# Neighbour counts from signs made by ScalarE, neighbour masks in halves by TensorE

## The chip, the cores and the metric

One NeuronCore of a Trainium2 chip runs the whole program. The metric is the device time of one execution in microseconds; runs of one kernel are compared by their median. Engines are named as in the profile: TensorE (PE, with its weight loads PEld), VectorE (DVE), ScalarE (ACT), GpSimd (POOL), and SyncE (SP), which issues the DMAs.

## The reference

The input is 16 graphs ("elements") of 1024 nodes with 64 features each, and a dense 0/1 adjacency. Four layers follow one another; each normalizes the features, clips them at zero and adds its result to its input. The change lies in layer 0. There each node's neighbours are thinned (of more than ten, every skip-th is removed, in either direction), and for every feature three quantiles over the values of the remaining neighbours are taken and weighted:

```python
removed = nb & do_dil[..., None] & ((rank + 1) % skip[..., None] == 0)
rem = removed | jnp.swapaxes(removed, 1, 2)
adj_d = jnp.where(rem, 0.0, adj_)                     # adj_: with self loops
...
vals = jnp.where(valid[..., None], x[:, None, :, :], big)   # valid = adj_d > 0
sv = jnp.sort(vals, axis=2)
for tau, wt in zip([0.25, 0.5, 0.75], [0.25, 0.5, 0.25]):
    pos = jnp.clip(tau * (m - 1.0), 0.0)
    lo, hi = floor(pos), ceil(pos)
    agg = agg + wt * (sv[lo] * (1 - frac) + sv[hi] * frac)
```

A two-layer network on x + agg ends it. Layer 1 is a weighted mean over the adjacency, layer 2 an attention of eight heads with the adjacency as a bias, layer 3 a product with the adjacency and a weight.

## The kernel before

Nothing of size (nodes x nodes x features) is sorted. The values of each feature are ranked once per element (`ranks`, a sorting network on VectorE for two elements at a time). A rank is split by `places` into one of 64 buckets (`bk`) and a place among the 16 in it (`pw`, a power of two). For every pair of features `pair_weights` builds two tables of 128 source nodes x 8 chunks x 64 buckets x 2 features: `cw` is 1 where the bucket's number is above the node's bucket, `dw` is the difference of place words between adjacent buckets. `group` multiplies both with the neighbour mask `valid` on TensorE (512 columns, eight matmuls each): `pc` is then the number of neighbours below each bucket, `pword` the bit word of the places in it. ScalarE takes `pc` out of PSUM as `cum`, `pword` as `hi`, `c1` and `c0`.

A step (b, g, t, q) serves an element, a group of eight features, a half of the 1024 columns, and one of six positions (floor and ceiling of three quantiles); an element has 8 x 2 x 6 = 96 steps. `compare` finds the bucket by `le = cum <= krow[q]` and picks count, word and value by matmuls (`prep`, `val`); `bits` and `value` finish one and two steps later. `krow[q]` comes from `positions`: the matmul `pm` of ones with `valid` counts the neighbours, and ScalarE scales the count to the position.

`picks` is a generator over these 1536 steps. Six steps ahead of need it starts `make`, which runs `group` for the next half piece by piece; `pair_weights` is called in the halves t = 0, four times. Beside it `behind` runs `background` for the next element: a part of the ranking, and `dilate`, the thinning of the eight chunks of 128 rows. `dilate` writes two arrays to DRAM: `left_d`, the neighbours that the row itself keeps, transposed by TensorE (`pv`) and copied out by ScalarE, and `rem_d`, those that the row removes. At the end of an element `stages` prepares the next one: `places`, then `neighbours` (both arrays are read back, and VectorE writes `valid = left > rem` as one fp8 tile of 1024 columns), `positions`, and `sorted_table`. The first stage is taken twelve steps before the element's end, the second seven, the others one a step.

A second generator, `layers`, does layers 1 to 3 of the finished element. After each step of `picks` it is advanced by 0.42 units of work; so layer matmuls and copies are emitted between the steps. The tile framework then orders the instructions of each engine by priority and readiness when the program is built; `adjoining` keeps the matmuls of one group together. Buffers come from small rotating tags: `b2` (six buffers, shared by sort, thinning and masks), `a2` (four), `cw` (eight, for `cw` and `dw`), and in PSUM `pa`, `pb` and `pc` with two banks each.

After the last step the layers of the last element run alone.

Of the kernel before, what the change touches and what calls it, by code (L numbers as in the profile page):

```python
# [29 lines left out]
TOP = 2.0 ** 23  # L30
MID = 1600.0
UP = 4096.0
BASE = 1032.0
LOW = 2048.0


# [1 line left out]
def tile_preln_adj_stack(  # L38
# [54 lines left out]
    def b2_(name, shape=(P, 512), dt=F32):  # L93
        return sb.tile(list(shape), dt, tag="b2", bufs=6, name=name)
# [53 lines left out]
    nc.vector.tensor_copy(rev, rev_a)  # L148
    rev_d = dram.tile([P, C], HP, name="rev_d")
    nc.sync.dma_start(rev_d, rev)  # L150
    not_i = const.tile([P, P], BF, name="not_i")
    nc.vector.tensor_scalar(not_i, identf, -1.0, 1.0, op0=OP.mult, op1=OP.add)

# [5 lines left out]

    dif_k = const.tile([P, P], BF, name="dif_k")  # L160
    nc.vector.scalar_tensor_tensor(dif_k, fmp, 2.0, identf, op0=OP.is_equal, op1=OP.subtract)
    nc.vector.tensor_scalar(dif_k, dif_k, KHI, None, op0=OP.mult)
    nc.vector.memset(dif_k[:, 0:2], 0.0)
    less_h = const.tile([P, P], HP, name="less_h")
    nc.vector.tensor_scalar(less_h, identf, -LOW, None, op0=OP.mult)
# [102 lines left out]
    nc.vector.memset(mid_c[:, 0:1], MID)  # L268
    nc.vector.memset(mid_c[:, 1:2], MID * LOW)
    nc.vector.memset(mid_c[:, 2:3], -MID)  # L270


    up_c = const.tile([P, 3], F32, name="up_c")
    for i, shift in enumerate((-0.375, 0.375, 0.0)):
        nc.vector.memset(up_c[:, i : i + 1], BASE + shift)

    sel_q = const.tile([P, NQ, 2 * BKW], BF, name="sel_q")
    for q in range(NQ):
# [158 lines left out]
    def dilate(b):  # L437

        left_d = dram.tile([C, P, N], BF, name="left_d")
        rem_d = dram.tile([C, P, N], HP, name="rem_d")
        for c in range(C):
            blk = slice(c * P, (c + 1) * P)
            nb = b2_("nb", (P, N), BF)
            nc.vector.tensor_scalar(nb, adj_rows(b, c), 0.0, None, op0=OP.is_gt)
            nc.vector.tensor_tensor(nb[:, blk], nb[:, blk], not_i, OP.mult)
            cum = b2_("cumn", (P, N), HP)  # L450
            nc.vector.tensor_tensor_scan(cum, nb, nb, 0.0, OP.add, OP.max)
            m = cum[:, N - 1 : N]
            do = small("do", [P, 1])
            nc.vector.tensor_scalar(
                do, m, float(T_THRESH), mask[:, b * C + c : b * C + c + 1], op0=OP.is_gt, op1=OP.mult
            )
            mi = small("mi", [P, 1], I32)
            nc.vector.tensor_scalar(mi, m, 1.0, None, op0=OP.add)
            nc.vector.tensor_scalar(mi, mi, 1, None, op0=OP.logical_shift_right)


            sk = small("sk", [P, 3])
            nc.vector.tensor_scalar(sk[:, 0:1], mi, 1.0, do, op0=OP.add, op1=OP.mult)
            nc.vector.tensor_scalar(sk[:, 1:2], sk[:, 0:1], -1.5, 1.5, op0=OP.mult, op1=OP.add)
            nc.vector.tensor_scalar(sk[:, 2:3], sk[:, 0:1], 0.5, -0.5, op0=OP.mult, op1=OP.add)
            act(cum, cum, AF.Abs, bias=sk[:, 1:2])
            yield
            rem = b2_("rem", (P, N), HP)
            nc.vector.tensor_scalar(rem, cum, sk[:, 2:3], None, op0=OP.is_equal)
            nc.vector.tensor_tensor(rem, rem, nb, OP.mult)  # L470
            nc.sync.dma_start(rem_d[c], rem)
            nc.vector.tensor_tensor(nb, nb, rem, OP.subtract)
            nc.vector.tensor_tensor(nb[:, blk], nb[:, blk], ident, OP.add)
            yield
            pt = pb("pv", (P, C, P), BF)
            adjoining(
                nc.tensor.transpose(pt[:, j, :], nb[:, j * P : (j + 1) * P], ident)
                for j in range(C)
            )
            left = b2_("left", (P, C, P), BF)  # L480
            nc.scalar.copy(left, pt)
            nc.sync.dma_start(left_d[:, :, blk].rearrange("c p i -> p c i"), left)
            yield
        yield left_d, rem_d

    def neighbours(left_d, rem_d):
        valid = sb.tile([P, C, N], F8, tag="valid", bufs=1, name="valid")
        for j in range(C):
            left = b2_("left", (P, N), BF)
            nc.sync.dma_start(left, left_d[j])  # L490
            rem = b2_("rem", (P, N), HP)
            nc.sync.dma_start(rem, rem_d[j])
            nc.vector.tensor_tensor(valid[:, j, :], left, rem, OP.is_gt, saturate=False)  # L493
        return valid

    def ranks(V):

# [99 lines left out]
    def positions(valid):  # L597

        m1 = sb.tile([P, N], I16, tag="m1", bufs=1, name="m1")
        for t in range(NH):
            pm = pa("pm")
            adjoining(
                nc.tensor.matmul(
                    pm, ones, valid[:, j, t * 512 : (t + 1) * 512], start=j == 0, stop=j == C - 1
                )
                for j in range(C)
            )  # L610
            nc.vector.tensor_scalar(m1[:, t * 512 : (t + 1) * 512], pm, -1.0, None, op0=OP.add)
        yield None
        krow = []
        for q in range(NQ):

            krow.append(sb.tile([P, N], HP, tag="krow", bufs=NQ, name="krow"))
            act(
                krow[q], m1, AF.Identity, scale=(q // 2 + 1) / 4.0, bias=up_c[:, q % 2 : q % 2 + 1]
            )
            if q < NQ - 1:  # L620
                yield None
        n6 = a2("n6", (P, N), I16)
        nc.vector.tensor_scalar(n6, m1, q_tau, q_add, op0=OP.mult, op1=OP.add)
        nc.vector.tensor_scalar(n6, n6, 2, None, op0=OP.logical_shift_right)
        kq = sb.tile([P, N], HP, tag="kq", bufs=1, name="kq")
        nc.scalar.copy(kq, n6)
        yield krow, kq
        nr = a2("nr", (P, N), I16)
        nc.vector.tensor_scalar(nr, m1, r_tau, None, op0=OP.mult)
        nc.vector.tensor_scalar(nr, nr, 3, None, op0=OP.bitwise_and)  # L630
        coef = sb.tile([P, N], BF, tag="coef", bufs=1, name="coef")
        nc.vector.tensor_scalar(coef, nr, w_frac, w_one, op0=OP.mult, op1=OP.add)
        yield coef
# [33 lines left out]
    def pair_weights(c0, bk, pw):  # L667


        sh = [P, C, NBK, 2]  # L670
        ib = bc(iota_b[:, None, :, :], sh)
        b_ = bc(bk[:, :, None, c0 : c0 + 2], sh)
        cw = sb.tile(sh, BF, tag="cw", bufs=8, name="cw")
        nc.vector.tensor_tensor(cw, ib, b_, OP.is_gt)
        eq = a2("eq", sh, BF)
        nc.vector.tensor_tensor(eq, ib, b_, OP.is_equal)
        nc.vector.tensor_tensor(at[:, :, 1:, :], eq, bc(pw[:, :, None, c0 : c0 + 2], sh), OP.mult)
        dw = sb.tile(sh, BF, tag="cw", bufs=8, name="dw")
        nc.vector.tensor_tensor(dw, at[:, :, 1:, :], at[:, :, :NBK, :], OP.subtract)  # L679
        return cw, dw  # L680

    def group(g, t, bk, pw, valid, weights):
# [2 lines left out]

        hs = slice(t * 512, (t + 1) * 512)
        cum = tb("cum", (P, 4, 512), HP)
        c1 = tb("c1", (P, 4, 512), HP)  # L690
        c0 = tb("c0", (P, 4, 512), HP)
# [7 lines left out]
        for pp in range(4):  # L699
            if t == 0:  # L700
# [1 line left out]
            cw, dw = (w.rearrange("p c b s -> p c (b s)") for w in weights[pp])  # L702
            pc = pc_("pc")
            adjoining(
                nc.tensor.matmul(pc, cw[:, j, :], valid[:, j, hs], start=j == 0, stop=j == C - 1)  # L705
                for j in range(C)
            )
            act(cum[:, pp, :], pc, AF.Identity, bias=up_c[:, 2:3])
            if late is not None:
                low_part(*late)  # L710
            pw_ = pc_("pword")
            adjoining(
                nc.tensor.matmul(  # L713
                    pw_, dw[:, j, :], valid[:, j, hs], start=j == 0, stop=False, skip_group_check=True
                )
                for j in range(C)
            )
# [9 lines left out]
    def picks():  # L727
# [8 lines left out]
        weights, tables, state, vs_of, els = {}, {}, {}, {}, {}  # L736

        def make(el, g, t):
            gen = group(g, t, el.bk, el.pw, el.valid, weights)
            tables[el.b, g, t] = next(gen)  # L740
            return gen

        def compare(n):
# [2 lines left out]
            hs = slice(t * 512, (t + 1) * 512)  # L746
            cum, c1, c0 = tables[b, g, t]
            le = a4("le", (P, 4, 512), HP)
            nc.vector.tensor_tensor(le, cum, bc(el.krow[q][:, None, hs], [P, 4, 512]), OP.is_le)  # L749
            wa = a4("wa", (P, 4, 512), HP)  # L750
            nc.vector.tensor_tensor(wa, le, c0, OP.mult)  # L751
            wb = a4("wb", (P, 4, 512), HP)
# [66 lines left out]
        for _ in make(els[0], 0, 0):  # L819
            yield 0.1  # L820
        coming = behind = stages = iter(())
        last, per = len(steps), NG * NH * NQ
        for n in range(last + 2):
            b, g, t, q = steps[min(n, last - 1)]
            to_go = per - n % per
            if n < last:
# [3 lines left out]
                if to_go == 2 * NQ and b + 1 < B:  # L830
# [3 lines left out]
                        pass  # L834
                    els[b + 1] = arrive(b + 1)
                    stages = els[b + 1].stages
                    next(stages)
                if to_go <= NQ:
                    next(stages, None)
                if q == 0 and n + NQ < last:  # L840
                    coming = make(els[steps[n + NQ][0]], *steps[n + NQ][1:3])
            if 0 <= n - 1 < last:
                bits(n - 1)
            next(coming, None)
            if to_go == NQ + 1:
                next(stages, None)
            if 0 <= n - 2:
                value(n - 2)
                if (n - 1) % per == 0:
# [81 lines left out]
    def stages(el):  # L931
# [4 lines left out]
        nc.sync.dma_start(rk, rk_d[:, :, rows])  # L936
        el.bk, el.pw = places(rk)
        yield
        el.valid = neighbours(*thinned.pop(b))
        where = positions(el.valid)  # L940
        next(where)
        yield
        vs = q4("vs")
        nc.sync.dma_start(vs[rows, :], vs_d[rows, :])
        table = sorted_table(s, vs)
        for q in range(NQ - 1):
            next(where)
            if q == 2:
                next(table)
            yield  # L950
        el.krow, el.kq = next(where)
        el.tab = next(table)
# [253 lines left out]
```

## Time and profile before

| | |
|---|---|
| runs, median of 3 | 13935.4 us (13928.6 to 13939.7) |
| profiled execution, its time | 13956.7 us |
| its span | 13954.9 us |
| mean granted TensorE clock | 0.978 |
| TensorE busy | 12582.4 us, 90% |
| VectorE busy | 12588.9 us, 90% |
| ScalarE busy | 8441.5 us, 60% |
| DMA | 842 MB, 18.9% of the 16 engines |

The first step of an element begins when its first `le` (line 749) starts. The first of all starts at 323.9 us; before that the ranking and thinning of element 0 run with nothing beside them. From 13589 us on only the layers of the last element run. In between an element takes some 840 us. Rows of the profile give a line, an engine, an operation, the tiles as out<-in, the form, the count, then busy time and the mean duration of one, then the idle time before it and what ended it. ScalarE's activations and copies made through the helper `act` all have line 373, so they are told apart by their tiles.

### The profile page before, as it was taken

What the parts mean: (1) busy time and instruction counts of PE and PEld (TensorE: products, weight loads), DVE (VectorE), ACT (ScalarE), POOL (GpSimd) and SP (SyncE); (2) the same over time, 40 slices, a digit from 0 to 9 for tenths busy, and PEclk for the clock granted to TensorE, in tenths of its full rate; (3) what the DMA queues carried; (4) which work ended last, traced back from release to release, by engine and by line L of the source; (5) the groups of instructions that cost most, each with busy time, mean ns of one, the idle gap of its engine ahead of it and who ended that gap; (6) DMA issues with size and microseconds to landing.
All of it is one profiled execution on the core that took longest, in us unless ns stands there. A gap on an engine that the chain in (4) does not pass through costs nothing. (4 is left out here: it accounts for less than half of the span.)

```text
span 13954.9 us, 237846 instructions
## 1 busy us (share of the span) xinstructions
PE 12582.4 (90%) x95489; PEld 5956.5 (43%) x95489; DVE 12588.9 (90%) x22771; ACT 8441.5 (60%) x14490; POOL 24.4 (0%) x138
## 2 busy tenths in 40 slices
PE   1889999999999998999999999999989999999998
PEld 0224444444444444444444444444444444444445
DVE  9999999999998999999899998999989999878773
ACT  1446666666666665666566666666656666666656
POOL 0000000000000000000000000000000000000000
PEclk9999999999999999999999999999999999999998
DMA  3012121211212112121211212112121221201012
GB/s 98 28 35 68 46 81 50 79 55 54 75 49 85 50 55 73 52 80 51 65 59 52 87 47 78 48 60 77 48 77 49 66 68 47 90 27 61 25 43 76
DMA packets 482773, 842.39 MB, mean 60 GB/s; under 512 B 234624, under 2 KB 236800, under 8 KB 481664
## 3 DMA queue, kind: packets, MB, share of 16 engines
q1 hardware_dynamic: 481664, 827.18, 18.9%
q8 instruction: 748, 12.26, 0.4%
q14 instruction: 361, 2.96, 0.1%
HBM read 616.27 MB, written 206.57 MB: 59 GB/s over the span
## 5 line engine op out<-in xcount | busy, mean ns | idle before, releaser
L713 PE MATMUL pword<-valid,dw 128*128 128x512 fp8e4 x8192 | 1977.6, 384 | 139.0 <-DVE dw L679 101.8
L751 DVE TENSOR_TENSOR wa<-le,c 128x2048 f16<-128x2048 f16 x1536 | 1871.4, 1218 | 199.2 <-PE prep L765 170.3
L705 PE MATMUL pc<-valid,cw 128*128 128x512 fp8e4 x8192 | 1977.5, 382 | 18.6 <-DVE valid L493 14.7
L749 DVE TENSOR_TENSOR le<-cum,krow 128x2048 f16<-128x2048 f16 x1536 | 1869.4, 1217 | 36.2 <-PE val L765 36.1
L753 DVE TENSOR_TENSOR wb<-le,c 128x2048 f16<-128x2048 f16 x1536 | 1870.0, 1217 | 3.1 <-PE prep L765 3.1
L373 ACT ACTIVATE s<-s,nm 128x1024 f32<-128x1024 f32 x1024 | 1169.2, 1143 | 723.1 <-DVE nm L1099 718.9
L772 ACT COPY wi<-prep 128x512 f32<-128x512 f32 x1536 | 898.4, 585 | 773.0 <-PE prep L765 649.2
L373 ACT ACTIVATE hi<-pword,mid_c 128x512 f16<-128x512 f32 x1024 | 705.2, 689 | 1047.8 <-PE pword L718 1043.2
L713 PEld LDWEIGHTS <-dw 128*128 128x128 bf16 x8192 | 759.9, 98 | 1257.0 <-issue 220.8
L426 PE MATMUL pcols<-identf,s 128*128 128x128 f32 x8192 | 1151.9, 282 | 143.0 <-ACT s L373 93.7
L1090 PE MATMUL sp<-kT,qT 64*128 64x512 f32 x4096 | 1168.3, 646 | 123.4 <-DVE nm L1099 121.6
L705 PEld LDWEIGHTS <-cw 128*128 128x128 bf16 x8192 | 765.6, 98 | 1078.8 <-issue 252.2
L765 PE MATMUL val<-le,tab 128*32 128x512 f16 x12288 | 1136.1, 388 | 52.4 <-DVE vs L793 34.2
L426 PEld LDWEIGHTS pcols<-identf,s 128*128 128x128 f32 x8192 | 909.9, 142 | 627.0 <-ACT s L373 254.1
L793 DVE SCALAR_TENSOR_TENSOR vs<-pz,vs 128x512 f32<-128x512 f32 x1536 | 1050.1, 684 | 123.4 <-PE pz L786 96.9
L1109 PE MATMUL ao<-eT,v 128*64 128x128 f32 x16384 | 1121.5, 278 | 42.1 <-ACT eT L429 38.2
L429 ACT COPY eT<-pcols 128x512 f32<-128x512 f32 x2048 | 1108.9, 592 | 54.0 <-PE pcols L426 52.6
L373 ACT ACTIVATE cum<-pc,up_c 128x512 f16<-128x512 f32 x1024 | 707.6, 691 | 700.5 <-PE pc L705 669.2
L1109 PEld LDWEIGHTS ao<-eT,v 128*64 128x64 f32 x16384 | 920.9, 137 | 342.4 <-ACT eT L429 216.3
L373 ACT ACTIVATE vs<-val 128x512 f32<-128x512 f32 x1536 | 925.8, 603 | 203.0 <-PE val L765 106.7
L765 PE MATMUL prep<-wb,sel_w 128*32 128x512 f16 x6144 | 658.8, 395 | 204.2 <-DVE wb L753 197.8
L1099 DVE CUSTOM_DVE_ANT_0 s<-sp,ad,nm 128x512 f32<-128x512 f32 x1024 | 730.2, 746 | 88.9 <-PE sp L1090 88.3
(258 smaller groups left out, 19483.3 us busy)
## 6 DMA issues: line engine op xcount, KB each, us to landing
ad<-in_adj_dram SPq DMA_DIRECT2D x768, 512.0 KB
adjT_d<-aT SPq DMA_DIRECT2D x128, 512.0 KB
aT<-adjT_d SPq DMA_DIRECT2D x128, 512.0 KB
md<-sm SPq DMA_DIRECT2D x216, 256.0 KB
sb<-md SPq DMA_DIRECT2D x216, 256.0 KB
rem_d<-rem SPq DMA_DIRECT2D x128, 256.0 KB
left_d<-left SPq DMA_DIRECT2D x128, 256.0 KB
left<-left_d SPq DMA_DIRECT2D x128, 256.0 KB
```

Source lines behind the costliest of these rows:

```text
L373: nc.scalar.activation(out_, in_, func, **kw)
L426: nc.tensor.transpose(pt[:, c, :], ad[:, (4 * s + c) * P : (4 * s + c + 1) * P], identf)
L429: nc.scalar.copy(aT[:, 4 * s : 4 * s + 4, :], pt)
L705: nc.tensor.matmul(pc, cw[:, j, :], valid[:, j, hs], start=j == 0, stop=j == C - 1)
L713: nc.tensor.matmul(pw_, dw[:, j, :], valid[:, j, hs], start=j == 0, stop=False, skip_group_check=True)
L749: nc.vector.tensor_tensor(le, cum, bc(el.krow[q][:, None, hs], [P, 4, 512]), OP.is_le)
L751: nc.vector.tensor_tensor(wa, le, c0, OP.mult)
L753: nc.vector.tensor_tensor(wb, le, c1, OP.mult)
L765: nc.tensor.matmul(dst[32 * pp : 32 * pp + 32, :], w[pp], r[pp], start=i in (0, 3), stop=i in (2, 4), tile_position=(0, 32 * pp),)
L793: nc.vector.scalar_tensor_tensor(vs, pz, -191.0, vs, op0=OP.is_equal, op1=OP.mult)
L1090: nc.tensor.matmul(sps[e], qT[e * D : (e + 1) * D, i * P : (i + 1) * P], kT[e * D : (e + 1) * D, hs], start=True, stop=True,)
L1109: nc.tensor.matmul(ao[e * D : (e + 1) * D, :], v[:, j, e * D : (e + 1) * D], eTs[e][:, j, :], start=j == 0, stop=j == C - 1, tile_position ...
```

## The change

Three things are done together.

1. `pair_weights` subtracts once (`cw` = bucket number minus the node's bucket). `eq` is then a comparison of `cw` with zero, and ScalarE turns `cw` in place into a sign: `Sign(0.5 - cw)`, which is +1 or -1. A sum of signs over the neighbours is (total - 2 x count below), so `group` takes `cum` out of PSUM as half the sum, by a Copy with scale 0.5 instead of an Identity with a bias column, and `compare` asks `is_ge` against a `krow` in the same halves (scale 0.5 - tau, bias 0.5 or -0.25). `dif_k` changes its sign. The constant columns `up_c` go, `half_c` comes.

2. `dilate` writes `left_d` as it lies, without the transpose; `rem` is bf16. `neighbours` is called for one half of the columns at a time and yields after each of the eight chunks. For a chunk it reads four blocks of `left_d` and half a row block of `rem_d` into one tile `lr`; TensorE forms the mask in PSUM: one matmul with minus the identity on `rem`, four with the blocks of `left` as weights on the identity, which transposes them; ScalarE writes `valid` by a Relu. There are two `valid` tiles of 512 columns.

3. The stages are spread: instead of one lump seven steps before the end, a table `STEPS` says how many pieces to take at each of the last twelve steps.

```diff
+    minus_i = const.tile([P, P], BF, name="minus_i")
+    nc.vector.tensor_scalar(minus_i, identf, -1.0, None, op0=OP.mult)
...
-    nc.vector.tensor_scalar(dif_k, dif_k, KHI, None, op0=OP.mult)
+    nc.vector.tensor_scalar(dif_k, dif_k, -KHI, None, op0=OP.mult)
...
-    up_c = const.tile([P, 3], F32, name="up_c")
-    for i, shift in enumerate((-0.375, 0.375, 0.0)):
-        nc.vector.memset(up_c[:, i : i + 1], BASE + shift)
+    half_c = const.tile([P, 3], F32, name="half_c")
+    for i, shift in enumerate((0.5, -0.25, 0.5)):
+        nc.vector.memset(half_c[:, i : i + 1], shift)
...
-        rem_d = dram.tile([C, P, N], HP, name="rem_d")
+        rem_d = dram.tile([C, P, N], BF, name="rem_d")
...
-            rem = b2_("rem", (P, N), HP)
+            rem = b2_("rem", (P, N), BF)
...
-            pt = pb("pv", (P, C, P), BF)
-            adjoining(
-                nc.tensor.transpose(pt[:, j, :], nb[:, j * P : (j + 1) * P], ident)
-                for j in range(C)
-            )
-            left = b2_("left", (P, C, P), BF)
-            nc.scalar.copy(left, pt)
-            nc.sync.dma_start(left_d[:, :, blk].rearrange("c p i -> p c i"), left)
+            nc.sync.dma_start(left_d[c], nb)
...
-    def neighbours(left_d, rem_d):
-        valid = sb.tile([P, C, N], F8, tag="valid", bufs=1, name="valid")
+    def neighbours(left_d, rem_d, t):
+        hs = slice(t * 512, (t + 1) * 512)
+        valid = sb.tile([P, C, 512], F8, tag=f"valid{t}", bufs=1, name="valid")
         for j in range(C):
-            left = b2_("left", (P, N), BF)
-            nc.sync.dma_start(left, left_d[j])
-            rem = b2_("rem", (P, N), HP)
-            nc.sync.dma_start(rem, rem_d[j])
-            nc.vector.tensor_tensor(valid[:, j, :], left, rem, OP.is_gt, saturate=False)
-        return valid
+            lr = b2_("lr", (P, 2, 512), BF)
+            nc.sync.dma_start(
+                lr[:, 0, :].rearrange("i (c j) -> i c j", c=4),
+                left_d[4 * t : 4 * t + 4, :, j * P : (j + 1) * P].rearrange("c i j -> i c j"),
+            )
+            nc.sync.dma_start(lr[:, 1, :], rem_d[j, :, hs])
+            pn = pb("pn")
+            def made():
+                yield nc.tensor.matmul(
+                    pn, minus_i, lr[:, 1, :], start=True, stop=False, skip_group_check=True
+                )
+                for c in range(4):
+                    cols = slice(c * P, (c + 1) * P)
+                    yield nc.tensor.matmul(
+                        pn[:, cols], lr[:, 0, cols], ident, start=False, stop=c == 3,
+                        skip_group_check=True,
+                    )
+            adjoining(made())
+            act(valid[:, j, :], pn, AF.Relu, saturate=False)
+            if j < C - 1:
+                yield None
+        yield valid
...
-                    pm, ones, valid[:, j, t * 512 : (t + 1) * 512], start=j == 0, stop=j == C - 1
+                nc.tensor.matmul(pm, ones, valid[t][:, j, :], start=j == 0, stop=j == C - 1)
...
-        yield None
+            yield None
...
-                krow[q], m1, AF.Identity, scale=(q // 2 + 1) / 4.0, bias=up_c[:, q % 2 : q % 2 + 1]
+                krow[q], m1, AF.Identity, scale=0.5 - (q // 2 + 1) / 4.0,
+                bias=half_c[:, q % 2 : q % 2 + 1],
...
-        nc.vector.tensor_tensor(cw, ib, b_, OP.is_gt)
+        nc.vector.tensor_tensor(cw, ib, b_, OP.subtract)
         eq = a2("eq", sh, BF)
-        nc.vector.tensor_tensor(eq, ib, b_, OP.is_equal)
+        nc.vector.tensor_scalar(eq, cw, 0.0, None, op0=OP.is_equal)
+        act(cw, cw, AF.Sign, scale=-1.0, bias=half_c[:, 2:3])
...
-            act(cum[:, pp, :], pc, AF.Identity, bias=up_c[:, 2:3])
+            act(cum[:, pp, :], pc, AF.Copy, scale=0.5)
...
-            nc.vector.tensor_tensor(le, cum, bc(el.krow[q][:, None, hs], [P, 4, 512]), OP.is_le)
+            nc.vector.tensor_tensor(le, cum, bc(el.krow[q][:, None, hs], [P, 4, 512]), OP.is_ge)
...
+        STEPS = {12: 1, 11: 2, 10: 2, 9: 2, 8: 2, 7: 5, 6: 4, 5: 1, 4: 1, 3: 1, 2: 1, 1: 2}
...
-                    next(stages)
-                if to_go <= NQ:
+                for _ in range(STEPS.get(to_go, 0)):
                     next(stages, None)
...
-            if to_go == NQ + 1:
-                next(stages, None)
...
-        el.valid = neighbours(*thinned.pop(b))
+        masks = thinned.pop(b)
+        el.valid = []
         where = positions(el.valid)
-        next(where)
-        yield
+        for t in range(NH):
+            for r in neighbours(*masks, t):
+                if r is None:
+                    yield
+            el.valid.append(r)
+            next(where)
+            yield
         vs = q4("vs")
         nc.sync.dma_start(vs[rows, :], vs_d[rows, :])
         table = sorted_table(s, vs)
+        next(table)
+        yield
         for q in range(NQ - 1):
             next(where)
-            if q == 2:
-                next(table)
             yield
```

More of the change, by code (lines that the diff above doesn't have):

```diff
@@ L32 @@
 UP = 4096.0
-BASE = 1032.0
 LOW = 2048.0
@@ L605, in positions @@
             adjoining(
-                nc.tensor.matmul(
-                    pm, ones, valid[:, j, t * 512 : (t + 1) * 512], start=j == 0, stop=j == C - 1
-                )
+                nc.tensor.matmul(pm, ones, valid[t][:, j, :], start=j == 0, stop=j == C - 1)
                 for j in range(C)
@@ L682, in group @@
     def group(g, t, bk, pw, valid, weights):
-        hs = slice(t * 512, (t + 1) * 512)
         cum = tb("cum", (P, 4, 512), HP)
@@ L704, in group @@
             adjoining(
-                nc.tensor.matmul(pc, cw[:, j, :], valid[:, j, hs], start=j == 0, stop=j == C - 1)
+                nc.tensor.matmul(pc, cw[:, j, :], valid[:, j, :], start=j == 0, stop=j == C - 1)
                 for j in range(C)
             )
-            act(cum[:, pp, :], pc, AF.Identity, bias=up_c[:, 2:3])
+            act(cum[:, pp, :], pc, AF.Copy, scale=0.5)
             if late is not None:
@@ L713, in group @@
                 nc.tensor.matmul(
-                    pw_, dw[:, j, :], valid[:, j, hs], start=j == 0, stop=False, skip_group_check=True
+                    pw_, dw[:, j, :], valid[:, j, :], start=j == 0, stop=False, skip_group_check=True
                 )
@@ L738, in make @@
         def make(el, g, t):
-            gen = group(g, t, el.bk, el.pw, el.valid, weights)
+            gen = group(g, t, el.bk, el.pw, el.valid[t], weights)
             tables[el.b, g, t] = next(gen)
```

## The prediction

> A measurement of this kernel can tell about 0.2% (28 us) from no change; "faster" and "slower" below mean by more than that.
>
> **What bounds the kernel now.** I read the page's head first. TensorE and VectorE are both busy for 90% of the span, so the shares alone don't say which sets the time, and the change takes work from VectorE and gives some to TensorE.
>
> ```profile
> span 13954.9 us, 237846 instructions
> PE 12582.4 (90%) x95489; PEld 5956.5 (43%) x95489; DVE 12588.9 (90%) x22771; ACT 8441.5 (60%) x14490; POOL 24.4 (0%) x138
> ```
>
> The kernel holds its own experiment. The sort and its way back for the next pair of elements stop at 11754 us (last row of line 563) and the thinning at 12144 us (last row of line 469), while elements 14 and 15 are still to come. I asked for the busy times by element, cut where the first `le` (line 749) of each begins (columns: stretch, length, busy PE, PEld, DVE, ACT, POOL, TensorE clock, DMA share, GB/s). They are elements 4, 5, 14 and 15.
>
> ```profile
> 3524.80:4368.90 844.10, 781.89 (x5990) 370.82 (x5988) 795.31 (x1402) 530.11 (x912) 1.77 (x8) 0.98 0.20 63
> 4368.90:5197.80 828.90, 772.89 (x5919) 364.92 (x5917) 767.30 (x1427) 521.66 (x900) 1.53 (x8) 0.99 0.20 62
> 11918.70:12754.30 835.60, 783.83 (x5962) 369.97 (x5962) 697.80 (x1216) 526.24 (x904) 1.55 (x8) 0.98 0.17 53
> 12754.30:13589.00 834.70, 773.87 (x5949) 367.88 (x5947) 641.48 (x1094) 503.82 (x883) 1.49 (x8) 0.98 0.13 40
> ```
>
> The reader is to see that VectorE falls from 795 to 641 us while the element takes 829 to 844 us before and 835 after. TensorE stays at 93 to 94% of each. So **TensorE, with the waits between its bursts, sets the pace**, and VectorE's load is near to it but not above it. Elements 4 and 5 speak a little against this: 28 us of VectorE go with 15 us of time.
>
> Then I read the waits of TensorE (who waited for whom, total us, times, longest), to see what stands between its bursts and which of it the change touches.
>
> ```profile
> PE prep L765 <- DVE wb L753: 197.8, 192, 5.2
> PE pword L713 <- DVE dw L679: 101.8, 93, 3.4
> PE pcols L426 <- ACT s L373: 93.7, 116, 3.0
> PE pm L606 <- DVE valid L493: 27.7, 23, 5.0
> PE pc L705 <- DVE valid L493: 14.7, 31, 1.7
> ```
>
> Last I read the order of time around one call of `pair_weights` (start, duration).
>
> ```profile
> 4335.93 0.68 DVE L674 TENSOR_TENSOR cw<-iota_b,bk 128x1024 bf16<-128x1024 bf16 x1
> ...
> 4340.92 1.90 PE L705 MATMUL pc<-valid,cw 128*128 128x512 fp8e4 x8
> ...
> 4341.71 0.69 DVE L676 TENSOR_TENSOR eq<-iota_b,bk 128x1024 bf16<-128x1024 bf16 x1
> ...
> 4344.12 0.68 DVE L679 TENSOR_TENSOR dw<-at 128x1024 bf16<-128x1024 bf16 x1
> ...
> 4345.21 1.04 PE L713 MATMUL pword<-valid,dw 128*128 128x512 fp8e4 x4
> ```
>
> Here `cw` is made early and the eight matmuls of `pc` run before `eq` has begun; `pword` then waits for `dw`. The change breaks this order: the Sign overwrites `cw` in place, so it can't start before `eq` has read it, and `pc` comes after the Sign.
>
> **What the Trainium skill says.** "VectorE: DVE Perf Modes", The perf-mode tier table: a two-tensor operation in bf16 reaches two elements a cycle, a one-tensor operation four. The trace agrees in kind: 684 ns for the two-tensor `cw`, 479 ns for the one-tensor `rem` (line 469) of the same size. "ScalarE: Activation LUTs", What ACT_TABLE_LOAD costs: 186 ns + 0.833 ns an element, and about 93 ns for each per-partition operand. The trace: 603 ns for a Copy of 512 (estimate 613), 691 ns with a bias column (estimate 706). The same page, Table sets: cheap functions sit in every set; it names relu, copy, identity and abs there, not sign. The trace has 34 table loads of 1283 ns and none for Abs, but no Sign. "Perfetto Trace Analysis", Identifying the Most-Contended Engine: matmul busy time is no good measure of headroom, since matmuls are pipelined; hence the comparison of elements above rather than the 90%.
>
> **The change part by part.** The rows that price it (busy us, mean ns of one):
>
> ```profile
> L373 ACT ACTIVATE cum<-pc,up_c 128x512 f16<-128x512 f32 x1024 | 707.6, 691 | 700.5 <-PE pc L705 669.2 <-DVE le L749 15.9 <-DVE bit L780 4.9
> L493 DVE TENSOR_TENSOR valid<-left,rem 128x1024 fp8e4<-128x1024 bf16 x128 | 153.4, 1220 | 27.4 <-DMA rem<-rem_d 19.0 <-PE pword L713 7.9 <-issue 0.2
> L373 ACT ACTIVATE cumn<-cumn,sk 128x1024 f16<-128x1024 f16 x128 | 147.4, 1152 | 146.5 <-DVE sk L464 135.4 <-DVE sk L465 10.0 <-DMA aT<-adjT_d 0.8
> L481 ACT COPY left<-pv 128x1024 bf16<-128x1024 bf16 x128 | 129.3, 1010 | 89.8 <-PE pv L477 89.7
> L477 PE MATMUL pv<-ident,nb 128*128 128x128 bf16 x1024 | 85.8, 226 | 127.0 <-DVE nb L472 111.8 <-DVE nb L473 15.1
> L469 DVE TENSOR_SCALAR rem<-cumn,sk 128x1024 f16<-128x1024 f16 x128 | 61.3, 479 | 3.0 <-ACT cumn L373 3.0
> ```
>
> VectorE. `cw` becomes a subtraction of the same form: 684 ns, no change. `eq` becomes a one-tensor comparison with a constant. Nearest is `rem`'s 479 ns, less the per-partition scalar (lines 454 and 458 on one column take 207 and 144 ns): 479 - 60 = 420 ns. It saves 684 - 420 = 264 ns x 512 = 135 us. `valid` goes: 153 us. Together -288 us, 18 us an element. Elements 14 and 15 put this near zero; elements 4 against 5 would give 15/28 of it, -154 us. I take a tenth: **-29** (ends 0 and -154).
>
> ScalarE. Added: 512 Signs at 1152 ns (the Abs, same size, bias column) = 590 us; 256 Relus out of PSUM at 603 to 691 ns, 0.65 x 256 = 166 us. Removed: `left`, 129 us; `cum` as a Copy with a constant, 691 - 603 = 88 ns x 1024 = 90 us. Net +537 us: 60% busy becomes 64%. ScalarE isn't the bound, but TensorE waits for it in many places, about 300 us by summing its waits on ACT. If a wait grows as busy over idle (1.53 to 1.80), that is +18%, 54 us; since `cum` is also out of PSUM sooner, I take **+30** (ends 0 and +90).
>
> TensorE. Rates come from busy time over count, for the mean of a matmul includes its pipeline: 1977.6/8192 = 0.241 us for 512 columns, 85.8/1024 = 0.084 us for a transpose with its own weights. Each of the 256 masks (16 elements x 2 halves x 8) takes one of the first and four of the second; 1024 transposes of `pv` go. 256 x 0.241 + 1024 x 0.084 - 1024 x 0.084 = +62 us. TensorE idles some 7% of an element and the masks are spread over ten steps, so a fifth falls into gaps: **+50** (ends +20 and +70).
>
> The wait for masks. TensorE now stands 27.7 + 14.7 = 42 us for `valid`. Afterwards `pm` can still wait for the last Relu of each half, 32 x 0.65 = 21 us: **-22**. The mask matmuls wait for their reads (`lr`): twice as many reads as before, of half the size, in the same six-buffer tag, on SP's queue, behind which the adjacency rows of the layers are queued. VectorE waited 19 us on 21 of 128 such reads; twice as many on TensorE would be 38, none if they run ahead: **+10**. Writing `nb` as it lies instead of the transposed copy costs nothing: the 256-byte pieces move from the write to the read, and the DMA engines are 19% busy.
>
> The weights. `pword` waits for `dw` 93 times; each is 264 ns shorter: **-25**. At such places `pc` can no longer go ahead of `eq`: eight matmuls, 8 x 0.241 = 1.93 us, come after the Sign. After `eq`, `dw` needs two more operations, 2 x 684 ns = 1.37 us, the Sign 1.15 us, so both are ready about together and `pc` has lost its cover. 93 x 1.93 = 180 us if nothing else fills it, nothing if matmuls of the layers do; I take a sixth: **+30** (ends 0 and +180). Behind a Sign that waits for `eq`, ScalarE's evictions `hi`, `wi`, `vs` stand in line, and TensorE for their PSUM; that is the third rival.
>
> The start. Before the first `le` (323.9 us) nothing hides 16 Relus and the first Signs; 8 VectorE masks of 1.22 us go: **+5** (ends -10 and +15). Signs and offsets folded into constants, `is_ge` for `is_le`, bf16 for fp16 in `rem` and the steps of the stages cost nothing by themselves: same shapes, same rows.
>
> Sum: -29 + 30 + 50 - 22 + 10 - 25 + 30 + 5 = **+49 us**. The profiled execution took 13956.7 us (span 13954.9 and 1.8 around it), so 14006 by its clock. It lies 21 us above the median of the runs, 13935.4; against that, **13985 us**.
>
> **The rivals.**
> VectorE is the bound after all (faster). For it: 93 to 94% busy in elements 4 and 5, and the 28 us there that cost 15. Against: elements 14 and 15. It gives -154 + 49 + 29 = -76, about 13860, and 13755 if nine tenths of 288 us count. The other terms come to +78, so it decides from 106 us, 37% of VectorE's saving, on.
> It evens out (no change). Mask matmuls and `pc` drop into gaps that TensorE has anyway, +50 and +30 halved, and ScalarE's share hides: 49 - 25 - 15 - 30 = -21, 13914.
> ScalarE's queue blocks (clearly slower). If a third of the 512 Signs hold the queue for 1.15 us and TensorE behind it, +196 on top: 14180. For it: ACT already stands 719 us for `nm`, so its order runs into VectorE's. Against: it is idle 36%.
> The mask reads come late, 256 x 0.6 us = +154: 14140.
> The change does not do what it says: Sign is not in the loaded sets, and 512 Signs cost two loads each, 1024 x 1.283 = +1314 us: 15300.
>
> **How the numbers follow.** My forecast 0.30, VectorE 0.28, evens out 0.22, blocked queue 0.14, late reads 0.04, table loads 0.02. Slower: 0.30 + 0.14 + 0.04 + 0.02 = 0.50; no change 0.22; faster 0.28. The forecast is 13985, its own range 13964 to 14060. For 8 in 10 the range reaches through the VectorE case down to 13800 and up to 14180, leaving out the far half of that case and of the blocked queue.
>
> **What would show it.** In the changed profile: `eq` at about 420 ns, `cw` at 684; VectorE near 12300 us busy; Sign rows near 1150 ns and as many table loads as before; `cum` near 603 ns; TensorE's busy time up by some 60 us; waits of `pc` on ScalarE's `cw` in place of `pword` on `dw`; none on VectorE's `valid`. An element should take 838 to 842 us. If elements 1 to 13 fall by 10 us while 14 and 15 don't, VectorE was the bound and I am wrong; if all rise by over 15 us with ScalarE's waits on `eq`, it is the queue.

## The result, and the profile after

The changed kernel takes **13925.0 us** (median of 11 runs, 13916.7 to 13937.9) against 13938.7 us (11 runs, 13925.6 to 13962.1): ratio **0.9990, 95% interval 0.9981 to 0.9998**. That is 14 us less, half of what the prediction called the smallest difference to be told from none. The forecast was 50 us more: the sign was wrong, and the size of several terms.

The head of the changed kernel's page, its profiled execution:

```profile
span 13921.9 us, 238842 instructions
PE 12568.3 (90%) x95745; PEld 5943.7 (43%) x95745; DVE 12368.4 (89%) x22644; ACT 8885.4 (64%) x15130; POOL 27.0 (0%) x138
```

VectorE's busy time falls by 220 us, ScalarE's rises by 444, TensorE's falls by 14. The work was moved from VectorE to ScalarE as the change says; on TensorE, the new rows don't show in the sum. The rows of what came in, and one that stayed (busy us, mean ns of one, idle before it and who ended it):

```profile
L372 ACT ACTIVATE cum<-pc 128x512 f16<-128x512 f32 x1024 | 612.1, 598 | 683.0 <-PE pc L718 674.7 <-DVE bit L793 3.7 <-DVE le L762 1.6
L372 ACT ACTIVATE cw<-cw,half_c 128x1024 bf16<-128x1024 bf16 x512 | 591.0, 1155 | 80.7 <-DVE eq L688 79.8
L688 DVE TENSOR_SCALAR eq<-cw 128x1024 bf16<-128x1024 bf16 x512 | 214.1, 418 | 5.9 <-PE pz L798 5.1 <-DMA z<-w 0.4
L372 ACT ACTIVATE valid<-pn 128x512 fp8e4<-128x512 f32 x256 | 146.4, 599 | 75.8 <-PE pn L497 72.4 <-PE pword L726 1.4
L497 PE MATMUL pn<-ident,lr 128*128 128x128 bf16 x1024 | 101.6, 221 | 0.0
L492 PE MATMUL pn<-lr,minus_i 128*128 128x512 bf16 x256 | 99.2, 387 | 2.7 <-DMA lr<-rem_d 2.5
L372 ACT ACT_TABLE_LOAD x34 | 43.6, 1283 | 24.8 <-DVE rq_f L312 24.2
```

The prices hold: `eq` 418 ns (420 forecast), the Sign 1155 (1152), `cum` 598 (603), and 34 table loads as before, so Sign needs no switch. The mask reads are no wait (2.5 us).

The two profiled spans are 33 us apart, but 19 of these belong to the two executions and not to the change: the one of the kernel before took 18 us more than its median here (13956.7 against 13938.7), the one of the changed kernel 1 us less. Where the 33 us lie is seen by stage, cut at the first `le` of elements 0, 1 and 14 (columns as in the prediction). First the kernel before, then the changed one:

```profile
0.00:323.90 323.90, 39.43 (x172) 18.20 (x173) 294.77 (x738) 41.95 (x53) 1.50 (x11) 0.99 0.34 103
323.90:1034.80 710.90, 594.26 (x3572) 195.10 (x3572) 666.72 (x919) 311.34 (x498) 0.00 (x0) 0.93 0.10 32
1034.80:11918.70 10883.90, 10071.38 (x77371) 4786.90 (x77368) 10145.72 (x18352) 6835.00 (x11748) 18.82 (x104) 0.98 0.20 62
```

```profile
0.00:336.30 336.30, 39.90 (x195) 20.07 (x196) 286.92 (x737) 47.83 (x67) 1.50 (x11) 0.98 0.33 99
336.30:1008.40 672.10, 569.43 (x3569) 190.34 (x3568) 646.93 (x902) 336.96 (x535) 0.00 (x0) 0.95 0.11 34
1008.40:11899.00 10890.60, 10090.10 (x77591) 4781.07 (x77588) 9974.49 (x18248) 7196.89 (x12271) 21.38 (x104) 0.99 0.20 62
```

The start is 12 us longer, **element 0 is 39 us shorter**, and elements 1 to 13, most of the run, are 7 us longer in 10884 although VectorE is busy 171 us less in them. Element 14 gives 10 us, the rest 3. In element 0 no layers of a finished element run yet: TensorE is busy 84% there, VectorE 94%. So the profiled gain lies where VectorE is the busier of the two, and elsewhere its relief is spent on something. VectorE's load alone doesn't account for the 39 us: its busy time falls by only 20 there. A part is spread between executions: with the same work on VectorE and TensorE (the spare Signs below), element 0 took 703.5 us. The granted clock differs in it, too (0.93 and 0.95).

The elements that the prediction had compared (4, 5, 14, 15):

```profile
3507.50:4359.10 851.60, 783.78 (x5985) 369.14 (x5985) 783.43 (x1392) 555.95 (x946) 1.21 (x8) 0.98 0.20 63
4359.10:5191.40 832.30, 777.52 (x5972) 367.21 (x5972) 754.62 (x1416) 551.01 (x943) 2.10 (x8) 0.99 0.20 61
11899.00:12724.20 825.20, 772.89 (x5972) 365.97 (x5972) 681.45 (x1206) 554.72 (x945) 1.55 (x8) 0.99 0.17 53
12724.20:13556.00 831.80, 776.95 (x5958) 368.31 (x5957) 636.32 (x1096) 525.83 (x910) 1.49 (x8) 0.99 0.13 40
```

They are no shorter in 4 and 5, although VectorE now has 12 us less in each. What changed most, past the start, are TensorE's waits for the weights, the masks and the attention (who waited for whom, total us, times, longest):

```profile
PE sp L1109 <- DVE nm L1118: 189.4, 225, 3.3
PE pc L718 <- ACT cw L372: 81.5, 118, 9.4
PE pm L619 <- ACT valid L372: 9.6, 18, 1.3
```

The wait of `pword` for `dw` (102 us) and those for `valid` (42 us) are gone. In their place stand 82 us of `pc` for the Sign, and the attention's `sp` waits 68 us longer for VectorE's `nm`; before, that row was

```profile
PE sp L1090 <- DVE nm L1099: 121.6, 172, 3.9
```

How the first of these comes about, at one `pair_weights` of the changed kernel:

```profile
4747.71 0.68 DVE L686 TENSOR_TENSOR cw<-iota_b,bk 128x1024 bf16<-128x1024 bf16 x1
...
4758.35 0.42 DVE L688 TENSOR_SCALAR eq<-cw 128x1024 bf16<-128x1024 bf16 x1
4758.80 1.15 ACT L372 ACTIVATE cw<-cw,half_c 128x1024 bf16<-128x1024 bf16 x1 [1.85 <-DVE eq L688]
...
4760.01 3.21 PE L718 MATMUL pc<-valid,cw 128*128 128x512 fp8e4 x8 [1.83 <-ACT cw L372]
```

The subtraction has ended 10 us before `eq` reads it. `eq` comes late, the Sign must wait for it, ScalarE stands idle for 1.85 us and TensorE for 1.83. The 512 instructions of each kind can be paired in order of start (for `pc`, the first eight matmuls with each `cw`). Before, `pc` began ahead of `eq`'s end in 372 cases; now in none. The median from the end of the operation that makes `cw` to the start of `eq` is 6.9 us (5.7 before).

### The profile page after: what moved, and what is told of

The parts are those of the page before. It is cut to its first block, busy times and chain, and to the rows that moved or that the text cites. A ratio compares the mean times of both kernels' runs of the same rounds, so it can differ in the third digit from the quotient of the medians.

```text
span 13921.9 us, 238842 instructions
## 1 busy us (share of the span) xinstructions
PE 12568.3 (90%) x95745; PEld 5943.7 (43%) x95745; DVE 12368.4 (89%) x22644; ACT 8885.4 (64%) x15130; POOL 27.0 (0%) x138
## 5 line engine op out<-in xcount | busy, mean ns | idle before, releaser
L726 PE MATMUL pword<-valid,dw 128*128 128x512 fp8e4 x8192 | 1944.9, 380 | 18.0 <-ACT cum L372 15.8
L372 ACT ACTIVATE cum<-pc 128x512 f16<-128x512 f32 x1024 | 612.1, 598 | 683.0 <-PE pc L718 674.7
L1118 DVE CUSTOM_DVE_ANT_0 s<-sp,ad 128x512 f32<-128x512 f32 x1024 | 675.9, 684 | 161.7 <-PE sp L1109 131.5
```

The lines of the kernel that those rows point to most:

```text
L372: nc.scalar.activation(out_, in_, func, **kw)
L726: nc.tensor.matmul(pw_, dw[:, j, :], valid[:, j, :], start=j == 0, stop=False, skip_group_check=True)
```

## The experiments

Ratios are to the kernel before, run beside each version on the same chip, with 95% intervals. One limit holds for all of them: the framework orders the instructions anew for each version, so a change of load also changes the order, and no run holds the order fixed.

**The two halves of the change, and VectorE's relief alone.**

Signs alone: the kernel before with the new `pair_weights`, `cum`, `krow`, `le` and `dif_k`.

> The kernel before with the signs alone (one subtraction, eq from it, Sign by ScalarE, counts and positions in halves); thinning, masks and stages as before. VectorE does 135 us less, ScalarE 500 us more, TensorE the same. Theory A (TensorE with its waits sets the pace while layers run, so VectorE's relief shows only in element 0): elements 1 to 13 stay within 0.5% of 837 us each, element 0 falls by 10 to 20 us, the total by about 15 us (ratio 0.998 to 1.000). Rival B (VectorE's relief is worth its share everywhere and the masks' matmuls eat it): elements 1 to 13 fall by 5 to 8 us each, ratio 0.992 to 0.995. Rival C (the Sign is what costs, the masks pay for it): elements 1 to 13 rise by 4 us or more, ratio 1.003 or more.

Measured: 1.0005 (0.9996 to 1.0013).

Masks alone: the changed kernel with those edits undone.

> The changed kernel with the weights, counts and positions of the kernel before; masks in halves by TensorE and the stages spread as changed. VectorE does 153 us less, TensorE some 60 us more, ScalarE 40 us more. Theory A: elements 1 to 13 within 0.5% of 837 us, the start longer by 5 to 12 us, element 0 shorter by 15 to 25 us, ratio 0.998 to 1.000. Rival B (masks cost what VectorE's relief gains): elements 1 to 13 rise by 2 to 5 us each, ratio 1.002 to 1.006. Rival C (masks gain what the Sign costs): they fall by 4 us or more, ratio 0.994 to 0.997.

Measured: 1.0000 (0.9992 to 1.0009).

Cheap `eq`, on the kernel before:

```diff
-        nc.vector.tensor_tensor(eq, ib, b_, OP.is_equal)
+        nc.vector.tensor_scalar(eq, cw, 0.0, None, op0=OP.is_equal)
```

> The kernel before, only that eq is made by one one-tensor comparison of cw with zero (684 to 420 ns, 512 times: 135 us less of VectorE), nothing added on any other engine. It leaves out the right choice of the bucket: eq marks other buckets than it should. Theory A: elements 1 to 13 move by less than 2 us each, element 0 falls by 10 to 20 us, ratio 0.998 to 1.000. Rival B (VectorE's relief is worth its share): 135/16 = 8.4 us of each element, ratio 0.991 to 0.994.

Measured: **0.9968 (0.9956 to 0.9981)**.

`eq` twice, on the kernel before:

```diff
         nc.vector.tensor_tensor(eq, ib, b_, OP.is_equal)
+        nc.vector.tensor_tensor(eq, ib, b_, OP.is_equal)
```

> The kernel before with eq computed twice: 512 more VectorE operations of 684 ns, 350 us in all, 21.9 us an element. Theory A with VectorE just below the pace: elements 1 to 13 rise by 5 to 15 us (VectorE then is busy 816 of some 840 us and becomes the bound), element 0 by its full 22 us or more, ratio 1.006 to 1.018. If TensorE has room for it all: ratio below 1.004. Rival B (VectorE bounds already): 22 to 25 us each, ratio 1.025 or more.

Measured: **1.0112 (1.0098 to 1.0126)**.

What follows. VectorE's load does count: 135 us less gives 45 us (0.32%), a third; 350 us more costs 156 us (1.12%), 45%. (By VectorE's busy time in the profiles, 126 us less and 295 more, it is 36 and 53%.) In the profile of the cheap `eq`, element 0 is 23 us shorter, elements 1 to 13 together 32, element 14 8. Rival B had the whole of VectorE's relief; it is wrong in both runs. My theory A had next to nothing outside element 0 for the cheap `eq` (0.998 or more), and misses there; the doubled `eq` lies inside its range (1.006 to 1.018), with elements 1 to 13 longer by 9.7 us each. So near its present amount VectorE's load is worth a third to a half of itself. The intervals are 18 to 20 us wide to either side, so the third is anything from a fifth to nearly a half.

Each half of the change pays back what it gains, though the numbers that B gave for the halves didn't come: both stand at the upper end of A's range. The signs stand 0.37% above the cheap `eq`, which is all their relief and a little more; the masks relieve VectorE of 153 us and gain nothing. Each half alone shortens element 0 (693.9 and 684.7 us, from 710.9).

**What the Sign costs: ScalarE's load, or its place?**

On the kernel before, a Sign that nobody waits for:

```diff
         nc.vector.tensor_tensor(eq, ib, b_, OP.is_equal)
+        spare = sb.tile(sh, F8, tag="spare", bufs=1, name="spare")
+        act(spare, cw, AF.Sign, scale=-1.0, bias=up_c[:, 2:3], saturate=False)
```

> The kernel before, with 512 more Signs by ScalarE: each reads cw as it stands and writes a spare tile that nobody reads; nothing waits for it. ScalarE does about 590 us more, no other engine does more, no order is forced. The signs alone stood 0.37% (52 us) above the cheap eq alone. Theory L (that is ScalarE's load): ratio 1.003 or more. Theory D (that is the new order: pc behind eq and the Sign): ratio below 1.0015.

Measured: 1.0005 (0.9997 to 1.0013). 512 Signs more, 506 us of ScalarE's busy time, are free within 0.13%: theory L falls.

The signs alone without the Sign:

```diff
-        act(cw, cw, AF.Sign, scale=-1.0, bias=half_c[:, 2:3])
```

> The signs alone (masks as before), with the Sign left out, so that the counts are wrong. VectorE does 135 us less as with the cheap eq alone. Theory D (the Sign costs by its place: behind eq and ahead of pc): the 52 us between the signs alone (1.0005) and the cheap eq alone (0.9968) go, ratio 0.996 to 0.9975. If the other edits of the signs (subtraction, Copy, positions in halves) cost them: ratio 0.9995 to 1.001.

Measured: 0.9971 (0.9960 to 0.9982), the cheap `eq` again. So 0.34% of the signs' 0.37% is the Sign, and by the run above not its load: what is left is its place between `eq` and `pc`. TensorE's waits go with it: from the signs alone to this run, those of `pc` for the Sign fall from 104 us to none and those of `sp` for `nm` from 188 to 131, while `pword` waits for `dw` again, 88 us.

The changed kernel without the Sign (same edit):

> The changed kernel with the Sign left out, so that the weights are the bare differences and the counts are wrong; 590 us of ScalarE and the step between subtraction and pc go, all else stays. Theories L and D both: 40 to 60 us below the changed kernel, ratio to the kernel before 0.995 to 0.997. If it stays at 0.999, neither is the cost and the cheap eq gains only in the order of the kernel before.

Measured: 0.9990 (0.9973 to 1.0008). The interval is wide because of one of its 14 executions, 14087.8 us; the others lie between 13908.8 and 13919.3. The median of all is 13915.0 against 13944.2 of the kernel before beside it: 0.9979, some 15 us below the changed kernel, where 40 to 60 were expected. So in the changed kernel the Sign's place costs, as far as this tells, a third of what it costs in the signs alone. No run shows why.

Can the Sign be put apart from `eq`? On the changed kernel:

```diff
-        nc.vector.tensor_tensor(cw, ib, b_, OP.subtract)
-        eq = a2("eq", sh, BF)
-        nc.vector.tensor_scalar(eq, cw, 0.0, None, op0=OP.is_equal)
-        act(cw, cw, AF.Sign, scale=-1.0, bias=half_c[:, 2:3])
+        dif = a2("dif", sh, BF)
+        nc.vector.tensor_tensor(dif, ib, b_, OP.subtract)
+        act(cw, dif, AF.Sign, scale=-1.0, bias=half_c[:, 2:3])
+        eq = a2("eq", sh, BF)
+        nc.vector.tensor_scalar(eq, dif, 0.0, None, op0=OP.is_equal)
```

> The changed kernel, but the subtraction goes to a tile of its own and the Sign from there to cw, so neither has the Sign to wait for eq nor eq for anything but the subtraction. Same load on all engines. Theory D (order): the waits of pc for the Sign fall from 82 us to below 40, ratio to the kernel before 0.995 to 0.9975. Theory L (load): as the changed kernel, 0.9985 to 1.0. A third outcome: the extra tile in the four-buffer tag delays eq and others, ratio above 1.0.

Measured: 1.0064 (1.0051 to 1.0077), slower, the third outcome; the wait of `pc` for the Sign rose from 82 to 113 us instead of falling. So this run doesn't test the Sign's place, for `dif` adds one more tile to the tag `a2`. Its `eq` row, and that of the kernel before, show on what `eq` waits:

```profile
L690 DVE TENSOR_SCALAR eq<-dif 128x1024 bf16<-128x1024 bf16 x512 | 217.1, 424 | 64.4 <-PE pz L798 63.4
L676 DVE TENSOR_TENSOR eq<-iota_b,bk 128x1024 bf16<-128x1024 bf16 x512 | 350.6, 685 | 29.8 <-PE pz L785 29.5
```

`pz` makes nothing that `eq` reads. It is the reader of `bit` and `wi`, which live in the same tag `a2` of four buffers: `eq` waits for a buffer. In the kernel before there were 29.5 us of such waits, which I had passed over.

**TensorE's part in the masks.** The changed kernel with one matmul for five:

```diff
-                yield nc.tensor.matmul(pn, minus_i, lr[:, 1, :], start=True, stop=False, ...)
-                for c in range(4):
+                for c in range(1):
                     cols = slice(c * P, (c + 1) * P)
-                    yield nc.tensor.matmul(pn[:, cols], lr[:, 0, cols], ident, start=False, ...)
+                    yield nc.tensor.matmul(pn, lr[:, 0, cols], lr[:, 1, :], start=True, stop=True, ...)
```

> The changed kernel with one matmul of 512 columns a mask instead of five (both read tiles still enter it), so that the masks are wrong; TensorE does 1024 transposes of 84 ns busy time less, 57 to 86 us, all waits stay. Theory A (TensorE sets the pace in elements 1 to 13): 40 to 70 us below the changed kernel, ratio to the kernel before 0.994 to 0.996. Rival (TensorE's extra work falls into its gaps): less than 20 us below, ratio 0.9975 to 0.999.

Measured: 0.9955 (0.9943 to 0.9967), 0.35% or 49 us below the changed kernel's 0.9990. That is what theory A said. The row removed had 102 us busy, and 57 to 86 us of work were expected to go. So TensorE's work counts for a half to five sixths of its busy time: also a part, not the whole.

**The buffer.** `eq` goes into the tile that becomes `dw` two operations later, instead of one of tag `a2`. Every engine does the same work.

```diff
-        eq = a2("eq", sh, BF)
+        dw = sb.tile(sh, BF, tag="cw", bufs=8, name="dw")
+        eq = dw
...
-        dw = sb.tile(sh, BF, tag="cw", bufs=8, name="dw")
```

On the changed kernel:

> The changed kernel with eq written into the buffer that dw gets afterwards (tag cw, eight buffers) instead of a tile of tag a2 (four, shared with wi, bit, w). Same work on every engine. In the changed kernel eq starts 6.9 us (median) after the subtraction has ended, and pc never before eq has. Theory D with the buffer as the cause: eq and the Sign move ahead, the wait of pc for the Sign falls from 82 to below 40 us, ratio to the kernel before 0.9945 to 0.9975. Rival (eq is late because VectorE is full, not for its buffer): ratio 0.998 to 1.0. Third: eq early takes VectorE from more urgent work, above 1.0.

Measured: **0.9781 (0.9768 to 0.9794)**, four times the gain expected at best.

On the kernel before:

> The kernel before with eq in dw's buffer in the same way: the control for the run above. There pc waits for cw alone, so eq's place matters only for dw and pword (102 us of waits). If the buffer matters through the Sign only: ratio 0.999 to 1.001. If it frees dw as well: 0.994 to 0.998.

Measured: **0.9762 (0.9749 to 0.9776)**. So the buffer is not a matter of the Sign. Its TensorE waits:

```profile
PE sp L1090 <- DVE nm L1099: 71.7, 110, 2.6
PE pword L713 <- DVE dw L679: 6.1, 8, 1.6
```

102 us of waiting for `dw` become 6, and 122 for `nm` become 72. With the same instructions the runs are 332 us shorter (the profiled spans 341). The pairs in order of start show what moved: from the end of `cw` to the start of `eq` the median falls from 5.7 to 1.1 us, and from the end of `dw` to the first `pword` matmul that reads it, it rises from 0.9 to 15.6 us. The weights had come just when TensorE needed them, or too late; now they lie ready. So these 2.4% were waiting, not the load of an engine, and another buffer for `eq`, with the order that the framework then makes, is what removed it. The granted clock is higher too, 0.984 against 0.978 to 0.981; if all of TensorE's time went with it, that would be some 0.5% (an estimate).

What in the buffer did it stays open. The edit lets `eq` come early, and it leaves the four buffers of `a2` to `wi`, `bit` and `w`, which are on the way of every step. No run separates the two, and none gives `a2` a fifth buffer. The run with `dif` is the counterpart: one tile more in `a2`, and 0.7% slower than the changed kernel.

**What the change is worth once the buffer is free.** Masks alone and signs alone, with `eq` in `dw`'s buffer.

> The masks in halves by TensorE and the spread stages, weights and counts as before, eq in dw's buffer. Against the kernel before with eq in dw's buffer (0.9762): if VectorE's relief is now worth more than the mask matmuls cost (50 us by the run with few masks), 0.972 to 0.975; if both cancel as they did with the shared tag, 0.975 to 0.978; if the masks cost, above 0.978.

Measured: 0.9789 (0.9776 to 0.9803).

> The signs alone, masks as before, eq in dw's buffer. If the Sign's price was its place behind a late eq, it is gone now and the cheap eq gains its 0.3%: 0.972 to 0.975. If the Sign still costs: 0.977 to 0.981.

Measured: **0.9743 (0.9730 to 0.9757)**, 13581.4 us, the fastest version. The head of its page, and one of its `pair_weights` (here `dw<-cw` is `eq`):

```profile
span 13575.8 us, 237190 instructions
PE 12264.6 (90%) x94441; PEld 5881.0 (43%) x95489; DVE 12458.6 (92%) x22771; ACT 8839.2 (65%) x15002; POOL 24.5 (0%) x138
```

```profile
4499.40 0.68 DVE L675 TENSOR_TENSOR cw<-iota_b,bk 128x1024 bf16<-128x1024 bf16 x1
4500.11 0.43 DVE L678 TENSOR_SCALAR dw<-cw 128x1024 bf16<-128x1024 bf16 x1
...
4500.57 1.15 ACT L373 ACTIVATE cw<-cw,half_c 128x1024 bf16<-128x1024 bf16 x1 [0.58 <-DVE dw L678]
...
4524.77 1.89 PE L708 MATMUL pc<-valid,cw 128*128 128x512 fp8e4 x8
```

`eq` follows the subtraction at once, and the Sign has ended 23 us before `pc` needs it (median of the 512: 23.9 us, against 0.5 in the changed kernel). ScalarE stands waiting for `eq` longer than in the changed kernel, 243 us against 80, but `pc` waits for the Sign only 14 us instead of 82. (TensorE's busy time in this head can't be compared with the other: of 95489 matmuls, about a thousand, almost all of one row of `pz`, left no record.) Against the kernel before with the same buffer (0.9762), the signs are 0.2% faster and the masks 0.3% slower; the intervals overlap or touch, so the two differences are likely rather than sure, while signs against masks (0.9743 and 0.9789) is clear. The whole change with the buffer (0.9781) is no faster than the kernel before with it: the change as it stands gains nothing there, and the signs alone are the part worth keeping.

## Why the prediction was wrong, point by point

**The bound.** "TensorE, with the waits between its bursts, sets the pace, and VectorE's load is near to it but not above it." The comparison of elements 4, 5, 14 and 15 showed that the pace didn't follow VectorE's load. It didn't show that it followed TensorE's, for all four elements shared the four-buffer tag `a2`. This is the step that failed in the mechanism: with `eq` out of that tag, the same TensorE work takes 2.4% less, so the "waits between its bursts" were not a fixed part of TensorE's pace. TensorE's work does count (49 us for 102 us busy), and so does VectorE's. And the comparison left out element 0, where VectorE is the busier engine and the profiled gain lies.

**"I take a tenth: -29 (ends 0 and -154)."** This is the term of the sum that was mis-sized most. The cheap `eq` alone measured a third; a third of 288 is -96, and that alone turns the sum of +49 into -18, the sign and about the size that was measured (-14). That it comes so near is luck, for the terms below were off as well, one way and the other. The tenth came from elements 14 and 15, the one pair that has 100 to 150 us less VectorE work than the rest. They show the mean over a large step, not the first 18 us of it. The other end, elements 4 against 5, gave over a half, and was a little nearer. The 288 us were too many, besides: they are the sum of two rows, but records of VectorE overlap (its durations summed fall by 323 us, its busy time by 220, because the overlap shrinks from 1702 to 1599).

**"I take +30" for ScalarE's load.** Measured: 7 us, interval -4 to +18. Going from 60 to 64% busy lengthened no wait that mattered.

**"I take a sixth: +30" with "-25" for the weights,** together +5. The order was foreseen (`pc` loses its lead over `eq`) and is in the trace; its size was not. In the signs alone the Sign's place costs 0.34%, 47 us; the 57 us by which `sp` waits longer were not foreseen. In the changed kernel it costs some 15 us. Why the two differ is not shown.

**The masks:** "+50", "-22" and "+10", with VectorE's share of 153 us. The waits for `valid` went from 42 to 10 us, as said to 21; the reads wait 2.5 us, not 10. TensorE's rows rose by 115 us (99 + 102 - 86), not 62: one matmul of 512 columns was busy for 387 ns here, where the forecast had 241 from bursts of eight, and a transpose 99 ns instead of 84. That TensorE's busy time as a whole still fell by 14 us is not explained. In the time, the masks alone cancel their own relief (1.0000).

**"The start: +5"** measured +12.

The measured parts don't simply add: the signs at +0.05% and the masks at 0.00% make -0.10% together. The intervals of each are about 0.1% wide, so this may be noise or the two helping each other; no run separates that. Neither of the signs that the prediction named at its end came: elements 1 to 13 took 837.7 us each (837.2 before), and it was element 14 that fell by 10.

Of the rivals, "it evens out" (13914) came closest in number; its mechanism, work dropping into TensorE's gaps, is not what the runs show, but relief and new waits of like size. The blocked queue exists at the Sign (80 us of ScalarE waiting for `eq`) but is far from its price of 196 us; in the fastest version ScalarE waits 243 us there, and it costs nothing that shows.

## What to carry to other kernels

When an instruction runs long after its inputs are there, and the rare waits ahead of it end with an engine that gives it no data, look for the buffer: here a four-buffer tag was shared with unrelated short-lived tiles while two engines stood at 90% busy, and moving one tile to a buffer that was going to be used anyway was worth 2.4%. Two engines at the same high share don't mean that one of them is the bound: measure what a little work is worth on each, by adding or removing some. Here an operation that was moved to an idle engine cost what it did to the order, not its own duration: the Sign in place had to wait for `eq`, the other reader of its tile, and `pc` for the Sign.

## What the runs showed of the hardware

With 512 Signs of 128x1024 added, the table loads stayed at 34. A one-tensor comparison in bf16 with a constant took 418 ns where the two-tensor one takes 684, and a two-tensor operation from bf16 into fp8 takes 1220 (the `valid` of the kernel before).
